# Layer 2 of a two-layer relational graph network on one core: several bunches in one PSUM bank, two banks for the projected sums, and finished blocks in steps

## The chip, the cores and the metric

The kernel runs on one core of one Trainium2 chip. The metric is the device time of one execution in microseconds. The engines are TensorE (PE, with PEld for its weight loads), VectorE (DVE), ScalarE (ACT), GpSimd (POOL, which here only issues gathers) and SyncE (SP, which issues most other transfers). Each engine works through its own instructions in order and waits on semaphores for the others.

## What is computed

12,500 nodes with 128 features, 200,000 edges sorted by destination, ten relations. The relation of an edge is the argmax of ten of its attributes.

```python
def _rgcn_layer(x, src, dst, edge_type, w_rel, root, bias):
    seg = dst * NUM_REL + edge_type
    sums = jax.ops.segment_sum(x[src], seg, num_segments=N * NUM_REL)
    cnt = jax.ops.segment_sum(jnp.ones(seg.shape, x.dtype), seg, num_segments=N * NUM_REL)
    mean = (sums / jnp.maximum(cnt, 1.0)[:, None]).reshape(N, NUM_REL, -1)
    return jnp.einsum('nrd,rdo->no', mean, w_rel) + x @ root + bias
h = jax.nn.relu(_rgcn_layer(x, src, dst, edge_type, w_rel1, root1, b1))
y = _rgcn_layer(h, src, dst, edge_type, w_rel2, root2, b2)
out = _layernorm(x + y, axis=-1)
```

## The kernel before

Layer 1 walks the edges in tiles of 128 and leaves three things in DRAM: `hT` (the hidden features, transposed), `YD` (each node's hidden features already multiplied by the ten relation matrices of layer 2, one row per node and relation), and `SD` (sums of hidden rows by relation and node, for edges that layer 1 itself could serve; they still have to be multiplied by layer 2's matrices). Layer 1 takes about two thirds of the time and isn't touched.

`layer_2` handles the edges that are left: 177 tiles in 45 bunches of up to 4 straight from the edge list ("plain" bunches), then 678 tiles of edges that were compacted meanwhile ("second" bunches of 1, 2 or 4 tiles that share one window of nodes), 261 bunches and 855 tiles in all. The accumulator `acc2` holds 128 features by 12,500 nodes in SBUF. The main loop runs over bunches p, with i counting tiles. In each turn the following is emitted, in this order:

1. DVE makes the weighted one-hot tiles of bunch p + 3 (`hots`, line 840); there are seven one-hot buffers. ACT starts blocks of the accumulator with `h @ root + bias` (`begun`, lines 1499 and 1500), with a PSUM tile `pf` from the pool `ps_f`, which has two buffers.
2. POOL gathers the bunch's rows of `YD`, one indirect transfer of 128 rows per tile (line 833), into six buffers of eight tiles. A buffer can be filled again when PE has read its eight tiles.
3. PE multiplies each gathered tile by its one-hot (line 1607) into the PSUM bank of this bunch: a plain bunch puts its tiles side by side, a second bunch accumulates its tiles on the same columns. Between the matmuls `between` runs what has fallen due at that tile.
4. While the compaction (`brought_together`) is under way, one of its steps.
5. DVE adds bunch p − 2 from its bank into `acc2` at an offset read from a register (line 1637; in the last four turns bunch p − 1).
6. Blocks of 128 or 256 nodes (51 of them, in the order `finals`) to which no later bunch adds are finished: PE transposes them (line 1540), DVE adds x and takes the row statistics (lines 773 to 777), ACT takes the root (line 779), DVE scales (lines 780 and 783), SP stores the rows and loads the x rows of the block three places on, into one of three buffers (line 698).

The banks: three `zy` while the compaction's masks hold three others; once they are closed, two `zq` more, so that bunches take five banks in turn, and one bank `alone`. From then on, every 12 tiles, one of 46 "heavy" blocks gets its part of `SD`: SP loads it (line 1513, 1280 KB, two buffers, the load for block j + 2 issued after the last matmul of block j), PE makes ten matmuls with the relation matrices into `alone` (line 1521, spread over 7 tiles), and DVE adds the result into `acc2` 9 tiles after the first of them (line 1528). A heavy block can be finished only after that.

Of the kernel before, what the change touches and what calls it, by code (L numbers as in the profile page):

```python
# [49 lines left out]
HB = 4  # L50
SPLIT = 64
LEAD = 40
LAST = 40
READY = 5
NEAR = 4
# [13 lines left out]
def rgcn_resnorm_kernel(ctx: ExitStack, tc: tile.TileContext, x, src, dst, attr, w_rel1, root1, b1,  # L69
# [1349 lines left out]
    def layer_2():  # L1419
# [95 lines left out]
        def seen(j, i):  # L1515
            k = heavy[j]
            n0, n, _ = block(k)
            po = alone[0]

            def one(r):  # L1520
                nc.tensor.matmul(po[:, :n], wsb[1][:, r, :], sds[k][:, r, :n], start=(r == 0), stop=(r == NREL - 1))  # L1521
                if r == NREL - 1:
                    sds.pop(k)
                    seen_in(j + 2)

            def added(_):
                assert k in begin[:begins]
                nc.vector.tensor_tensor(acc2[:, n0:n0 + n], acc2[:, n0:n0 + n], po[:, :n], op=ALU.add)  # L1528
# [37 lines left out]
        for p in range(-AH, NB + BE):  # L1566
            if p == plain - AH:
                assert wanted[0] in ready
                masking.close()
                ps_n = fast.enter_context(tc.tile_pool(name="ps_n", bufs=1, space=PSUM))  # L1570
                banks[:] = [next_of("zp", banks) for _ in banks] + [ps_n.tile([P, YB], F32, name=f"zq{j}") for j in range(2)]
                turn_of_["zp"] = 0
                alone.append(ps_n.tile([P, YB], F32, name="alone"))
                for j in range(len(heavy)):
                    seen(j, i + 6 + 12 * j)
            if p + AH < NB:
# [11 lines left out]
            if p < NB:  # L1588
                second, t0, n, w = bunches[p]
                oh = ohs.pop(p)  # L1590
                zps[p] = zp = next_of("zp", banks)
                for j in range(n):
                    if made % GQ == 0:
                        g = next_of("g", gathers)
                        turn = used_[id(g)] = 1 - used_.get(id(g), 1)
                    at = GQ - 1 - made % GQ if turn else made % GQ
                    made += 1
                    t = t0 + j
                    if second:
                        gathered(g, at, YD[:, :], idxB[:, t:t + 1], 1)  # L1600
                    else:
                        gathered(g, at, YD[:NREL * (limit_of(t) + 1), :] if t >= T0 else YD[:, :], idxE[:, t:t + 1], 1)
                    gs[j] = g, at
                for j in range(n):
                    g, at = gs.pop(j)
                    o = 0 if second else j * w
                    nc.tensor.matmul(zp[:, o:o + w], g[:, at * C:(at + 1) * C], oh[:, j * w:(j + 1) * w],  # L1607
                                     start=not second or j == 0, stop=not second or j == n - 1)
                    between.run(issued[p] + j + 1)
                i = issued[p + 1]  # L1610
# [7 lines left out]
            if opened is None and wanted[0] in ready:  # L1618
                opened = i
                for j in range(2):  # L1620
                    seen_in(j)
            for q in [q for q in sorted(zps) if q <= p - (1 if p >= NB - 4 else BE)]:
                second, t0, n, w = bunches[q]
                for j in range(1 if second else n):
                    t = t0 + j
                    if (second, t) not in offs:
# [10 lines left out]
                    nc.vector.tensor_tensor(s, s, zps[q][:, j * w:(j + 1) * w], op=ALU.add)  # L1637
                del zps[q]
            todo.run(i)
            summed_to = min(zps, default=min(p + 1, NB))  # L1640
            while ended < NB2 and done_at[finals[ended]] <= summed_to and (finals[ended] in whole or finals[ended] not in heavy):
                finish(ended)
# [172 lines left out]
```

## Time and profile before

| | us |
|---|---|
| median of three runs | 3691.99 |
| lowest and highest | 3690.94, 3702.55 |
| the profiled execution | 3655.59 |
| its span, first to last instruction | 3653.8 |

The profile is of one execution. It lists for every instruction when it started, how long it took and, where the engine had been idle before, what ended the wait. "Idle before ... <-DVE cc L1528" is a wait that DVE's instruction of line 1528 ended; "issue" is a wait that the profile can't name or the time between instructions; "remote" is a wait that ended with a semaphore whose sender the profile didn't find. A matmul of float32 operands appears as two rows, with a weight load for each. Layer 2's gathers begin at about 2361 us and the last starts at 3618.6 us. In slices of a fortieth of the span (91 us) the page gives PE three to seven tenths after the first slice, DVE mostly three tenths in the last ten slices, and POOL six tenths almost throughout.

### The profile page before, as it was taken

What the parts mean: (1) busy time and instruction counts of PE and PEld (TensorE: products, weight loads), DVE (VectorE), ACT (ScalarE), POOL (GpSimd) and SP (SyncE); (2) the same over time, 40 slices, a digit from 0 to 9 for tenths busy, and PEclk for the clock granted to TensorE, in tenths of its full rate; (3) what the DMA queues carried; (4) which work ended last, traced back from release to release, by engine and by line L of the source; (5) the groups of instructions that cost most, each with busy time, mean ns of one, the idle gap of its engine ahead of it and who ended that gap; (6) DMA issues with size and microseconds to landing.
All of it is one profiled execution on the core that took longest, in us unless ns stands there. A gap on an engine that the chain in (4) does not pass through costs nothing. (4 is left out here: it accounts for less than half of the span.)

```text
span 3653.8 us, 38569 instructions
## 1 busy us (share of the span) xinstructions
PE 2254.1 (62%) x11125; PEld 1859.4 (51%) x11125; DVE 1994.0 (55%) x6434; ACT 514.6 (14%) x799; POOL 2294.6 (63%) x2430
## 2 busy tenths in 40 slices
PE   1556677677676767676667667733556566566534
PEld 0445565565555555555555555623445555555433
DVE  4646576867565757565656565428654333233333
ACT  1111121212121212122212121100000000000000
POOL 5663666666666666666666666566566666666664
PEclk7677877878888888887888877855667777677655
DMA  4553656555555555555656555531144444444322
GB/s 122 154 170 96 189 155 192 153 186 165 172 172 169 172 177 176 171 182 158 191 159 194 158 161 157 146 98 51 46 117 135 143 137 140 136 151 135 97 61 51
DMA packets 376423, 529.31 MB, mean 145 GB/s; under 512 B 55904, under 2 KB 283707, under 8 KB 376204
## 3 DMA queue, kind: packets, MB, share of 16 engines
q0 software_dynamic: 99552, 249.45, 23.9%
q1 hardware_dynamic: 249209, 264.48, 22.4%
q10 hardware_dynamic: 27443, 12.82, 1.2%
q8 instruction: 93, 1.52, 0.2%
q14 instruction: 126, 1.03, 0.1%
HBM read 372.75 MB, written 160.19 MB: 146 GB/s over the span
## 5 line engine op out<-in xcount | busy, mean ns | idle before, releaser
L833 POOL DMA_INDIRECT g<-XH,idxE x1386 | 1314.1, 948 | 737.7 <-issue 364.8
L1077 PEld LDWEIGHTS zp<-oh,g 128*128 128x128 f32 x5898 | 901.7, 229 | 407.3 <-DVE cc L866 201.5
L1077 PE MATMUL zp<-oh,g 128*128 128x120 f32 x5898 | 943.1, 317 | 247.3 <-DVE cc L866 159.0
L866 DVE TENSOR_TENSOR cc<-cc,zp 128x240 f32 (+1 forms) x1563 | 607.1, 388 | 787.1 <-remote 353.0
L833 POOL DMA_INDIRECT g<-YD,idxB x678 | 642.6, 948 | 339.8 <-issue 185.9
L934 PE MATMUL yb<-w,a 128*128 128x512 f32 (+1 forms) x576 | 345.2, 689 | 346.0 <-ACT ys L940 183.1
L840 DVE TENSOR_SCALAR oh<-bank,keyE,wE 128x120 f32<-128x120 f32 x1563 | 517.7, 394 | 0.0
L1521 PE MATMUL alone<-cc,w 128*128 128x256 f32 (+2 forms) x920 | 339.4, 485 | 136.4 <-DVE cc L1528 72.8
L1607 PEld LDWEIGHTS zy<-oh,g 128*128 128x128 f32 x1168 | 245.9, 273 | 222.5 <-DVE cc L1637 155.1
L1607 PE MATMUL zy<-oh,g 128*128 128x12 f32 (+30 forms) x1168 | 237.2, 330 | 197.3 <-DVE cc L1637 148.2
L940 ACT ACTIVATE ys<-yb 128x512 f32<-128x512 f32 (+2 forms) x291 | 153.0, 526 | 1334.4 <-remote 553.7
L934 PEld LDWEIGHTS yb<-w,a 128*128 128x128 f32 x576 | 110.8, 240 | 379.1 <-ACT ys L940 203.6
L1521 PEld LDWEIGHTS alone<-cc,w 128*128 128x128 f32 x920 | 195.3, 247 | 158.3 <-DVE cc L1528 76.5
L826 PE MATMUL pf<-cc,w 128*128 128x256 f32 (+2 forms) x1040 | 248.4, 396 | 15.1 <-issue 9.2
L833 POOL DMA_INDIRECT g<-in_x_dram,idxE x177 | 167.8, 948 | 135.7 <-PE zp L1077 59.3
L833 POOL DMA_INDIRECT g<-YD,idxE x177 | 168.6, 953 | 111.1 <-issue 60.6
L826 PEld LDWEIGHTS pf<-cc,w 128*128 128x128 f32 x1040 | 205.7, 212 | 49.3 <-issue 19.8
L795 ACT ACTIVATE cc<-zero 128x1280 f32<-128x1280 f32 x170 | 214.6, 1262 | 0.0
L840 DVE TENSOR_SCALAR oh<-columns,keyB,wB 128x45 f32<-128x45 f32 (+35 forms) x678 | 177.0, 336 | 0.2 <-issue 0.2
L1637 DVE TENSOR_TENSOR cc<-cc,zy 128x12 f32 (+24 forms) x306 | 58.9, 192 | 177.8 <-remote 145.5
L1607 PEld LDWEIGHTS zq<-oh,g 128*128 128x128 f32 x542 | 113.2, 258 | 30.8 <-issue 18.4
L1528 DVE TENSOR_TENSOR cc<-cc,alone 128x256 f32<-128x256 f32 (+2 forms) x46 | 18.6, 405 | 199.3 <-remote 159.0
(265 smaller groups left out, 1563.5 us busy)
## 6 DMA issues: line engine op xcount, KB each, us to landing
SD<-cc SPq DMA_DIRECT2D x41, 1280.0 KB
cc<-SD SPq DMA_DIRECT2D x41, 1280.0 KB
YD<-ys SPq DMA_DIRECT2D x194, 256.0 KB
m<-in_edge_attr_dram SPq DMA_DIRECT2D x48, 672.0 KB
g<-XH,idxE POOLq DMA_INDIRECT x1386
YD<-ys SPq DMA_DIRECT2D x97, 128.0 KB
XH<-hb SPq DMA_DIRECT2D x44, 256.0 KB
g<-YD,idxB POOLq DMA_INDIRECT x678
```

What stands on the lines that cost most here:

```text
L795: nc.scalar.activation(cc[:, l, h * H:(h + 1) * H, o:o + n], zero[:, None, :n].to_broadcast([P, H, n]), AF.Copy)
L826: nc.tensor.matmul(po[:, :n], wsb[l][:, r, :], sums[:, r], start=(r == 0), stop=(w is None and r == NREL - 1))
L833: nc.gpsimd.indirect_dma_start(out=g[:, j * C:(j + n) * C], out_offset=None, in_=table, in_offset=bass.IndirectOffsetOnAxis(ap=idx, axis=0))
L840: nc.vector.tensor_scalar(oh[:, j * m:(j + 1) * m], cols[:, :m], keys[:, j:j + 1], weights[:, j:j + 1], op0=ALU.is_equal, op1=ALU.mult)
L866: nc.vector.tensor_tensor(s, s, z, op=ALU.add)
L934: nc.tensor.matmul(yb[:h, :m], fin_a[k][:, b * P:b * P + h], wsb[1][:, r:r + m // C, :], start=True, stop=True)
L940: nc.scalar.activation(ys[:h, :m], yb[:h, :m], AF.Copy)
L1077: nc.tensor.matmul(zp[:, o + l * KW:o + (l + 1) * KW], g[:, (slot[j] + l) * C:(slot[j] + l + 1) * C], oh[:, j * KW:(j + 1) * KW], start=Tr ...
L1521: nc.tensor.matmul(po[:, :n], wsb[1][:, r, :], sds[k][:, r, :n], start=(r == 0), stop=(r == NREL - 1))
L1528: nc.vector.tensor_tensor(acc2[:, n0:n0 + n], acc2[:, n0:n0 + n], po[:, :n], op=ALU.add)
L1607: nc.tensor.matmul(zp[:, o:o + w], g[:, at * C:(at + 1) * C], oh[:, j * w:(j + 1) * w], start=not second or j == 0, stop=not second or j = ...
L1637: nc.vector.tensor_tensor(s, s, zps[q][:, j * w:(j + 1) * w], op=ALU.add)
```

## The change

Bunches share a bank. Ahead of the loop a list `bank_of` gives each bunch a bank and its first column there: a bunch goes behind the one before it as long as the bank's 512 columns hold it and it has no more than 8 tiles in all; a new bank is begun at two fixed places and for each of the last four bunches. After the compaction there is one `zq` instead of two, so four banks in turn. Sums of a bunch are now emitted when the bank in use is two further on, among the second bunches two bunches a turn unless the bank is three or more further on, and in the last four turns all at once.

Projected sums use two banks `alone` in turn, and the addition comes 20 tiles after the first matmul instead of 9.

Finishing a block is cut in three steps by tile count: the transposes 8 tiles after the block is complete (and not within 11 tiles of the last block's), the addition of x, the statistics, the root and the x load 9 tiles later, the scaling and the store 4 tiles after that. While the compaction runs, the middle step follows the transposes at once. In the last 32 tiles (`RUSH`) all follow each other at once.

```diff
+        TOGETHER = 8
+        bank_of, cols, tiles = [], YB, 0
+        for p, (second, _, n, w) in enumerate(bunches):
+            m = w if second else n * w
+            if cols + m > YB or tiles + n > TOGETHER or p in (plain - 3, plain) or p >= NB - 4:
+                bank_of.append((bank_of[-1][0] + 1 if bank_of else 0, 0))
+                cols, tiles = m, n
+            else:
+                bank_of.append((bank_of[-1][0], cols))
+                cols, tiles = cols + m, tiles + n
...
-                xbs[finals[j]] = next_of("x", xs)
+                xbs[finals[j]] = xs[j % len(xs)]
...
-            po = alone[0]
+            po = alone[j % 2]
...
-            between.at(i + 9, added)
-
-        def finish(j):
+            between.at(i + 20, added)
+
+        free_from, unscaled = [0], []
+
+        def finish(j, i):
...
-            pr = ps_f.tile([P, 4, C], F32, name="pf")
-            for b, h in subs:
-                nc.tensor.transpose(pr[:h, b, :], acc2[:, n0 + b * P:n0 + b * P + h], ident)
-            normed(k, xbs.pop(k), pr, (next_of("v", vs), next_of("o", os_)))
-            rows_in_turn(j + 3)
+            held = {}
+
+            def turned_rows(i):
+                held["pr"] = pr = ps_f.tile([P, 4, C], F32, name="pf")
+                for b, h in subs:
+                    nc.tensor.transpose(pr[:h, b, :], acc2[:, n0 + b * P:n0 + b * P + h], ident)
+                del pr
+                if jobs.due or i >= NG - RUSH:
+                    measured(i)
+                else:
+                    todo.at(i + 9, measured)
+
+            def measured(i):
+                while unscaled:
+                    unscaled[0](i)
+                pr, xb = held.pop("pr"), xbs.pop(k)
+                held["v"] = v = next_of("v", vs)
...
+                for p, s in spans(k):
+                    nc.vector.tensor_tensor(v[:p, s], pr[:p, s], xb[:p, s], op=ALU.add)
...
+                for p, s in spans(k):
+                    nc.scalar.activation(rstd[:p, s], mv[:p, s, 1], AF.Sqrt, bias=eps[:p])
+                rows_in_turn(j + 3)
+                unscaled.append(scaled)
+                if i < NG - RUSH:
+                    todo.at(i + 4, scaled)
+                else:
+                    scaled(i)
+
+            def scaled(_):
...
+                for p, s in spans(k):
+                    nc.vector.reciprocal(rstd[:p, s], rstd[:p, s])
...
+                rows_dma(o, out, k, True)
+
+            if i >= NG - RUSH:
+                todo.run(END)
+                turned_rows(i)
+            else:
+                at = max(i + 8, free_from[0])
+                free_from[0] = at + 11
+                todo.at(at, turned_rows)
...
-                banks[:] = [next_of("zp", banks) for _ in banks] + [ps_n.tile([P, YB], F32, name=f"zq{j}") for j in range(2)]
+                banks[:] = [next_of("zp", banks) for _ in banks] + [ps_n.tile([P, YB], F32, name="zq")]
...
-                alone.append(ps_n.tile([P, YB], F32, name="alone"))
+                alone += [ps_n.tile([P, YB], F32, name=f"alone{j}") for j in range(2)]
...
-                zps[p] = zp = next_of("zp", banks)
+                zp, col = zps[p] = (next_of("zp", banks) if not bank_of[p][1] else zps[p - 1][0]), bank_of[p][1]
...
-            for q in [q for q in sorted(zps) if q <= p - (1 if p >= NB - 4 else BE)]:
+            if p >= NB - 4:
+                due = [q for q in sorted(zps) if q < p]
+            else:
+                due = [q for q in sorted(zps) if bank_of[q][0] <= bank_of[p][0] - 2]
+                if p >= plain:
+                    due = due[:max(2, sum(bank_of[q][0] <= bank_of[p][0] - 3 for q in due))]
+            for q in due:
...
-                    nc.vector.tensor_tensor(s, s, zps[q][:, j * w:(j + 1) * w], op=ALU.add)
-                del zps[q]
+                    nc.vector.tensor_tensor(s, s, zp[:, col + j * w:col + (j + 1) * w], op=ALU.add)
```

More of the change, by code (lines that the diff above doesn't have):

```diff
@@ L52 @@
 LEAD = 40
+RUSH = 32
 LAST = 40
@@ new lines, in measured @@
+            def measured(i):
[3 more added lines that the diff above has]
+                held["v"] = v = next_of("v", vs)
+                held["mv"] = mv = small.tile([P, 4, 2], F32, name="mv")
+                held["rstd"] = rstd = small.tile([P, 4], F32, name="rstd")
+                for p, s in spans(k):
+                    nc.vector.tensor_tensor(v[:p, s], pr[:p, s], xb[:p, s], op=ALU.add)
+                for b, h in subs:
+                    st = small.tile([P, nc.vector.BN_STATS_DIM], F32, name="st")
+                    nc.vector.bn_stats(st[:h], v[:h, b, :])
+                    nc.vector.bn_aggr(mv[:h, b, :], st[:h])
+                for p, s in spans(k):
[6 more added lines that the diff above has]
+                    scaled(i)
@@ new lines, in scaled @@
+            def scaled(_):
+                if scaled not in unscaled:
+                    return
+                unscaled.remove(scaled)
+                v, mv, rstd = (held.pop(a) for a in ("v", "mv", "rstd"))
+                o = next_of("o", os_)
+                for p, s in spans(k):
+                    nc.vector.reciprocal(rstd[:p, s], rstd[:p, s])
+                for b, h in subs:
+                    nc.vector.tensor_scalar(o[:h, b, :], v[:h, b, :], mv[:h, b, 0:1], rstd[:h, b:b + 1],
+                                            op0=ALU.subtract, op1=ALU.mult)
+                rows_dma(o, out, k, True)
@@ L1605, in layer_2 @@
                     g, at = gs.pop(j)
-                    o = 0 if second else j * w
+                    o = col if second else col + j * w
                     nc.tensor.matmul(zp[:, o:o + w], g[:, at * C:(at + 1) * C], oh[:, j * w:(j + 1) * w],
@@ L1621, in layer_2 @@
                     seen_in(j)
-            for q in [q for q in sorted(zps) if q <= p - (1 if p >= NB - 4 else BE)]:
+            if p >= NB - 4:
[5 more added lines that the diff above has]
+            for q in due:
                 second, t0, n, w = bunches[q]
+                zp, col = zps.pop(q)
                 for j in range(1 if second else n):
@@ L1641, in layer_2 @@
             while ended < NB2 and done_at[finals[ended]] <= summed_to and (finals[ended] in whole or finals[ended] not in heavy):
-                finish(ended)
+                finish(ended, i)
                 ended += 1
```

## The prediction

> **What bounds the kernel now.** I read the page first, then the busy time of all engines in stretches of layer 2 (only its code changes), then the waits of each engine there, then the timeline around one stop.
>
> ```profile
> span 3653.8 us, 38569 instructions
> ## 1 busy us (share of the span) xinstructions
> PE 2254.1 (62%) x11125; PEld 1859.4 (51%) x11125; DVE 1994.0 (55%) x6434; ACT 514.6 (14%) x799; POOL 2294.6 (63%) x2430
> ```
>
> No engine is full. The stretches of layer 2 tell more (busy us and instructions of PE, PEld, DVE, ACT, POOL; all of POOL's are gathers):
>
> ```profile
> core 0: us, PE busy (x) PEld busy (x) DVE busy (x) ACT busy (x) POOL busy (x), PEclk, DMA share, GB/s
> 2388.00:2602.00 214.00, 72.39 (x290) 62.61 (x290) 133.32 (x341) 8.85 (x24) 141.18 (x148) 0.50 0.26 66
> 2602.00:2746.00 144.00, 87.92 (x393) 74.25 (x393) 79.89 (x369) 7.05 (x18) 83.23 (x88) 0.71 0.31 89
> 2746.00:3488.70 742.70, 446.89 (x2043) 386.97 (x2043) 249.51 (x1089) 25.59 (x69) 485.36 (x512) 0.72 0.45 133
> 3488.70:3619.60 130.90, 52.43 (x228) 48.33 (x227) 41.25 (x183) 2.36 (x8) 90.08 (x95) 0.50 0.24 61
> 3619.60:3653.80 34.20, 13.64 (x58) 11.98 (x58) 19.11 (x81) 2.07 (x7) 0.00 (x0) 0.50 0.16 33
> ```
>
> Time per gather: 214.0/148 = 1.446 us, 144.0/88 = 1.636, and in the long third stretch 742.7/512 = 1.451. There DVE is busy a third of the time and PE 60%. What POOL does between its gathers stands in its group for that stretch, and the stops themselves in its timeline:
>
> ```profile
> L833 POOL DMA_INDIRECT g<-YD,idxB x513 | 486.3, 948 | 260.9 <-issue 140.1 <-remote 84.9 <-PE zy L1607 18.1
> ```
> ```profile
> 2386.81 0.95 POOL L833 DMA_INDIRECT g<-YD,idxE  x1 [11.16 <-issue]
> ...
> 2450.39 0.94 POOL L833 DMA_INDIRECT g<-YD,idxE  x1 [7.46 <-remote]
> ...
> 3304.62 0.95 POOL L833 DMA_INDIRECT g<-YD,idxB  x1 [3.30 <-remote]
> ...
> 3488.83 0.95 POOL L833 DMA_INDIRECT g<-YD,idxB  x1 [3.18 <-PE zy L1607]
> ...
> 3522.89 0.95 POOL L833 DMA_INDIRECT g<-YD,idxB  x1 [4.27 <-remote]
> ```
>
> A gather takes 0.95 us and 0.30 of issue, so 1.25 in a row; the rest of the idle time, 260.9 − 140.1 = 120.8 us, is stops. From 3488.83 to 3522.89 are 34.06 us: 24 gathers (30.0) and a stop that costs 4.27 − 0.30 = 3.97 more. From 2386.81 to 2450.39 are 45 gathers and a stop of 7.46. The commonest run is 16 gathers: 20.0 + 3.0 = 23.0. So a stop grows with the run before it: 16 gathers cost 1.4375 us each, 24 cost 1.4154, 45 cost 1.25 + 7.16/45 = 1.409. What a stop is, one of them shows, with all engines:
>
> ```profile
> 3267.35 0.66 PE L1521 MATMUL alone<-cc,w 128*128 128x256 f32 x2
> ...
> 3268.00 0.66 PE L1499 MATMUL pf<-cc,root 128*128 128x256 f32 x2
> ...
> 3277.26 0.95 POOL L833 DMA_INDIRECT g<-YD,idxB  x1 [0.31 <-issue]
> 3281.33 0.52 SPq L1513 DMA_DIRECT2D cc<-SD  x1
> 3281.34 0.42 DVE L1528 TENSOR_TENSOR cc<-cc,alone 128x256 f32<-128x256 f32 x1 [13.80 <-remote]
> 3281.42 0.47 ACT L1500 ACTIVATE cc<-pf,b 128x256 f32<-128x256 f32 x1 [19.01 <-remote]
> 3281.61 0.95 POOL L833 DMA_INDIRECT g<-YD,idxB  x1 [3.40 <-remote]
> ```
>
> PE has finished line 1521's last matmul by 3268.0 and line 1499's by 3268.7. ACT, SP, DVE and POOL, which wait for these or for later ones, all go on at 3281.3 to 3281.6, about 13 us after the matmuls and 3 us after POOL's last gather. **PE's word that a matmul is done reaches the others late while POOL gathers back to back, and at once when POOL has stopped.** "Remote" is how the profile names it. Who loses by it, in the long stretch:
>
> ```profile
> DVE cc L1528 <- remote: 135.4, 13, 14.5
> DVE cc L1637 <- remote: 106.1, 15, 12.5
> DVE cc L773 <- remote: 72.2, 9, 15.2
> ```
> ```profile
> PE alone L1521 <- DVE cc L1528: 72.8, 11, 12.6
> ```
>
> DVE stands 313.7 us in front of the three operations that the change postpones; PE, out of one-hot tiles or of the bank `alone`, stands behind DVE. PE therefore advances only some 16 tiles per stop, and POOL, whose six gather buffers of 8 tiles PE must free, gets 16 gathers.
>
> **The change, part by part.** No part adds or drops an arithmetic instruction, a transfer or a byte; all move waits. Sums per tile are as before (171 in the long stretch, below).
>
> *Shared banks.* Before, bunch q is added up two bunches later, which by the loop is 6 tiles after its matmuls, and five banks of one bunch hold about 5 × 3.0 = 15 tiles. After, four banks of up to 8 tiles hold up to 32, and a sum comes, by the same loop, 9 to 18 tiles later, 12 in the mean.
>
> ```profile
> 2746.00:3488.70 742.70, 39.34 (x171) 0.72 0.45 133
> ```
>
> 512 gathers over these 171 additions of line 1637 is 3.0 tiles a bunch. At 1.45 us a tile the slack goes from 9 to 17 us, against waits of at most 12.5. In the first two stretches (three banks) the same holds, 8 tiles instead of 4 a bank.
>
> *Two `alone` banks, addition at 20 instead of 9.* Ten matmuls lie within 7 tiles, so DVE's slack goes from 3 tiles (4 us) to 14 (20 us), and PE still has 4 tiles before the bank comes round at 24. Waits were up to 14.5 us: they mostly go.
>
> *Finished blocks in steps.* Before, DVE waits for transposes issued just before: no slack. After, 9 tiles (13 us), and 4 more behind ACT's root. Behind the waiting DVE instruction stand the next one-hot tiles, then PE. On SP the x load now comes 9 tiles later and the store 13, in its one queue with the SD loads.
>
> ```profile
> SPq L698 <- DVE o L783: 60.5, 14, 18.3
> ```
>
> SP stands 60.5 us of the long stretch before such a store; standing further back, the stores hold it less. The x load has two blocks' time (51 blocks to 855 tiles, so 2 × 17 × 1.45 = 49 us); without that cover its 128 KB would cost DVE under 1 us at the rate shown under (b). I take 0 for both. `pf`, with two buffers, is held for 9 tiles; the other one serves line 1499, once in about 16 tiles.
>
> **What is late next.** With the last word from PE at tile S, DVE now gets to S + 9 or more, where it got to S + 0 (a block), + 3 or + 6; three bunches of one-hots carry PE 9 further. So PE gains some 8 tiles a stop, one gather buffer: **runs of 24 instead of 16**, 1.4154 us a gather. Longer runs hardly add: the 45 gathers bound it at 1.409. Stops don't vanish, because POOL needs PE's word too.
>
> The sum, against the profiled execution's 3655.59 us (1.8 outside its span):
> - long stretch: 512 × 1.4154 = 724.7, **−18.0**. Bounds: −6.7 (512 × 1.4375, only stops above 3.3 us go) and −21.3 (1.409).
> - 2388 to 2602: at 1.4154, 209.5, so −4.5 at most; DVE is busy 133 of 214 us with the list of the second half, which isn't touched. I take **−2**.
> - 2602 to 2746: at 1.4154, 124.6, so −19.4 at most, 0 at least; PE and DVE work there on that same list one after the other. Nearest to the stretch before: **−3**.
> - 3488.7 to 3619.6: runs are 24 already, **0**.
> - the end:
>
> ```profile
> 3622.04 0.42 DVE L773 TENSOR_TENSOR cc<-pf,x 128x256 f32<-128x256 f32 x1 [22.52 <-remote]
> ...
> 3625.70 2.00 PE L1607 MATMUL zy<-oh,g 128*128 128x82 f32 x8 [15.98 <-DVE cc L1637]
> ```
>
> DVE waits through the whole last run, and when it ends PE has 25 of the 855 tiles left (its 58 rows in the last stretch above, less 8 of transposes, two rows a tile). After, the last 32 tiles finish at once, as now, but by the loop the block in question comes 12 tiles later, and the one-hots with it. PE took some 14 us for the 25, from 3625.7 to 3639.9: 12 tiles less are −7 at most; I take **−3**, as the sums and blocks behind them stay.
>
> Sum −26: 3629.6 for an execution like the profiled one. The median of the runs shown is 3691.99, 36.4 above it; I take the same 26 off: **3666**.
>
> **Rivals.**
> (a) *Runs stay at 16*, because another chain of PE's word has less slack than I think (ACT's line 1499/1500, the 9 tiles of a block). Then −6.7, and 1 at the most elsewhere: **3684**. For it: ACT waited 19.01 us above.
> (b) *Slower: the SD loads come late.* SP issues the load for block j + 2 only on PE's word that block j is done, and PE needs it 17 tiles (24 us) later.
>
> ```profile
> DMA packets 928, 0.98 MB, mean 328 GB/s; under 512 B 16, under 2 KB 912, under 8 KB 928
> ```
> ```profile
> SPq L1513 <- remote: 253.6, 18, 19.0
> ```
>
> Between 3260 and 3263 one load flows at 328 GB/s: 1280 KB take 4 us, say 6 with its start, which leaves 18. The run quoted began 23 us before 3281.6, and the first late matmul ended at 3268.0, 9 us on; in a run and stop of 34 us the word can be late by 25. So a block that ends in the first 7 us of that time, 7/34 of 43, hence 8 or 9 loads, has its load up to 7 us late, and PE starts again only after it. From 3.1 us each it eats the 26; at 5 us each (+42) it gives **3708**.
> (c) *Stops vanish*: PE keeps close to the gathers, and its word, even late, comes before POOL needs it, six buffers on. Then 1.25 a gather: 120.8 of the long stretch, **3571**. Against it: the run of 45 ended in the longest stop of all.
> (d) *Banks count, not tiles.* The Trainium skill, Perfetto Trace Analysis, "Matmuls" under "Optimizing Tensor Performance", says that independent matmul groups should rotate through different PSUM banks so that emptying one overlaps the next; here a bunch no longer gets its own. As a mechanism of this kernel: four banks for bunches instead of five put PE behind DVE's sums, as three banks did before 2746. Half-way from 1.451 to the 1.517 of the first two stretches together (358.0/236) is +0.033 a gather, +17: **3709**. Against it: the sums of a bank are 12 tiles old when they are read, and PE's wait is for the one-hots and `alone`.
>
> **How the numbers follow.** Forecast 0.56, (a) 0.21, (b) 0.12, (c) 0.06, (d) 0.05. All bounds of the sum together are −52, 3640. The range goes from 3636 to 3706, leaving out (c), (d) and the worse half of (b). 0.3%, about what a measurement of this kernel can tell from no change, is 11 us: faster 0.62 (forecast, (c)), same 0.21, slower 0.17.
>
> **What would show it.** After: POOL's stops some 34 us apart and near 4.3 us; the DVE rows "L1528, L1637, L773 <- remote" well under the 313.7 us; 512 gathers of the long stretch in about 725 us. Stops still 23 us apart make (a) right; PE standing before line 1521 with SP's SD load just landed, (b); runs of 40 and more without a stop of 6 us, (c). The forecast is wrong at its root if PE's word is no longer late, or is late without regard to POOL's runs.

## The result, and the profile after

Before 3691.25 us, after 3701.57 us (medians of 12 runs each); the ratio is 1.0022, with a 95% interval of 1.0012 to 1.0032. The change makes no gain; it costs some 8 us. Forecast were 26 us less.

The profiled execution of the kernel after took 3693.38 us. Its page, and the stretches of layer 2 between the same gathers as in the prediction (columns as there):

```profile
span 3691.6 us, 38716 instructions
PE 2319.4 (63%) x11125; PEld 1901.6 (52%) x11125; DVE 1995.1 (54%) x6434; ACT 513.8 (14%) x799; POOL 2287.9 (62%) x2430
```
```profile
2409.00:2623.40 214.40, 69.56 (x294) 63.40 (x295) 125.81 (x329) 7.49 (x23) 140.32 (x148) 0.50 0.26 66
2623.40:2774.30 150.90, 94.00 (x390) 78.56 (x390) 87.06 (x383) 8.48 (x19) 83.19 (x89) 0.68 0.30 88
2774.30:3522.40 748.10, 480.96 (x2063) 405.16 (x2062) 248.78 (x1083) 24.99 (x67) 483.88 (x512) 0.70 0.44 131
3522.40:3656.10 133.70, 49.96 (x207) 47.19 (x208) 44.10 (x192) 2.36 (x8) 88.97 (x95) 0.50 0.23 60
3656.10:3691.60 35.50, 14.00 (x58) 12.04 (x57) 18.60 (x77) 2.36 (x8) 0.94 (x1) 0.50 0.18 40
```

The 512 gathers of the long stretch take 748.1 us, where 724.7 were forecast. (Executions differ by several us a stretch; a pair taken together is below.) Its waits in that stretch (us in total, times, longest), and POOL's group of gathers:

```profile
DVE cc L1707 <- remote: 103.7, 12, 13.6
PE alone L1533 <- issue: 102.1, 104, 2.6
DVE oh L841 <- remote: 91.7, 22, 11.6
PE zy L1670 <- issue: 82.5, 88, 2.5
DVE cc L1572 <- remote: 36.0, 6, 13.4
PE zq L1670 <- issue: 27.5, 23, 2.6
DVE cc L1540 <- remote: 14.4, 1, 14.4
```
```profile
L834 POOL DMA_INDIRECT g<-YD,idxB x512 | 483.9, 945 | 271.0 <-issue 143.8 <-remote 52.2 <-PE zy L1670 27.4
```

Lines 1707, 1540 and 1572 are the sums, the addition of `alone` and the first step of a block, which were 1637, 1528 and 773: their 313.7 us have become 154.1. PE's 72.8 us in front of the addition are 1.2. So the waits that the change was aimed at are half gone. (These rows are the waits called remote. With those that the profile puts down to some PE row, DVE's idle time before the three operations went from 462.9 us to 274.3, and before the one-hot tiles from 0.2 to 167.5; all its idle time in the stretch is 493 us in both.) In their place stand DVE in front of the one-hot tiles (line 841, 91.7 us) and PE with 212.1 us of "issue": time in which it waited for nothing that the profile shows. POOL's idle time is no shorter. Its stops, from its timeline:

```profile
3103.01 0.94 POOL L834 DMA_INDIRECT g<-YD,idxB  x1 [3.61 <-remote]
...
3126.38 0.94 POOL L834 DMA_INDIRECT g<-YD,idxB  x1 [3.71 <-PE alone L1533]
```

They lie 23.4 us apart, 16 gathers, as before: 29 of the 34 runs between stops in the long stretch have 16. What PE's issue time looks like, its timeline shows. POOL took up gathering at 3149.95 us:

```profile
3159.35 0.66 PE L1533 MATMUL alone<-cc,w 128*128 128x256 f32 x2
3159.85 0.32 PE L1670 MATMUL zy<-oh,g 128*128 128x50 f32 x2
3160.01 0.40 PE L1557 MATMUL pf<-ident,cc 128*128 128x128 f32 x2
3160.24 0.60 PE L1511 MATMUL pf<-cc,root 128*128 128x256 f32 x2
3160.68 0.41 PE L1670 MATMUL zy<-oh,g 128*128 128x51 f32 x2
3161.60 0.30 PE L1670 MATMUL zy<-oh,g 128*128 128x51 f32 x1 [0.51 <-issue]
3163.01 0.24 PE L1670 MATMUL zy<-oh,g 128*128 128x51 f32 x1 [1.12 <-issue]
3164.41 0.45 PE L1670 MATMUL zy<-oh,g 128*128 128x51 f32 x1 [1.16 <-issue]
3165.81 0.24 PE L1670 MATMUL zy<-oh,g 128*128 128x51 f32 x1 [0.95 <-issue]
3167.24 0.24 PE L1670 MATMUL zy<-oh,g 128*128 128x51 f32 x1 [1.19 <-issue]
3168.67 0.43 PE L1670 MATMUL zy<-oh,g 128*128 128x51 f32 x1 [1.18 <-issue]
```

From 3156 to 3161 us PE begins five or six rows in each us. Then it begins one row every 1.4 us, though DVE had made the four one-hot tiles of these rows by 3157.9 us and their gathers had been issued some 50 us earlier. Two rows belong to a tile, and the second, which needs nothing that the first didn't, comes 1.4 us behind it too, which a late word can't explain. **PE crawls.** The experiments ask what makes it crawl and what that is worth.

### The profile page after: what moved, and what is told of

Same layout as the page of the kernel before. It is cut to its first block, busy times and chain, and to the rows that moved or that the text cites. A ratio compares the mean times of both kernels' runs of the same rounds, so it can differ in the third digit from the quotient of the medians.

```text
span 3691.6 us, 38716 instructions
## 1 busy us (share of the span) xinstructions
PE 2319.4 (63%) x11125; PEld 1901.6 (52%) x11125; DVE 1995.1 (54%) x6434; ACT 513.8 (14%) x799; POOL 2287.9 (62%) x2430
## 5 line engine op out<-in xcount | busy, mean ns | idle before, releaser
L1078 PEld LDWEIGHTS zp<-oh,g 128*128 128x128 f32 x5898 | 914.2, 232 | 398.8 <-issue 177.4
L1078 PE MATMUL zp<-oh,g 128*128 128x120 f32 x5898 | 953.1, 319 | 230.4 <-DVE cc L867 135.8
L935 PE MATMUL yb<-w,a 128*128 128x512 f32 (+1 forms) x576 | 359.9, 716 | 380.5 <-ACT ys L941 206.5
L1670 PEld LDWEIGHTS zy<-oh,g 128*128 128x128 f32 x1366 | 296.3, 275 | 280.0 <-issue 149.6
L1670 PE MATMUL zy<-oh,g 128*128 128x12 f32 (+33 forms) x1366 | 285.6, 330 | 240.1 <-issue 130.4
L1533 PE MATMUL alone<-cc,w 128*128 128x256 f32 (+2 forms) x920 | 357.2, 493 | 104.5 <-issue 102.1
L827 PEld LDWEIGHTS pf<-cc,w 128*128 128x128 f32 x1040 | 209.4, 215 | 57.7 <-issue 23.3
L1707 DVE TENSOR_TENSOR cc<-cc,zy 128x12 f32 (+21 forms) x339 | 64.7, 196 | 253.2 <-remote 94.3
L1512 ACT ACTIVATE cc<-pf,b 128x256 f32<-128x256 f32 (+2 forms) x51 | 23.7, 465 | 700.1 <-remote 313.1
L1670 PEld LDWEIGHTS zq<-oh,g 128*128 128x128 f32 x344 | 75.1, 264 | 57.6 <-issue 47.9
```

What stands on the lines that cost most here:

```text
L827: nc.tensor.matmul(po[:, :n], wsb[l][:, r, :], sums[:, r], start=(r == 0), stop=(w is None and r == NREL - 1))
L935: nc.tensor.matmul(yb[:h, :m], fin_a[k][:, b * P:b * P + h], wsb[1][:, r:r + m // C, :], start=True, stop=True)
L1078: nc.tensor.matmul(zp[:, o + l * KW:o + (l + 1) * KW], g[:, (slot[j] + l) * C:(slot[j] + l + 1) * C], oh[:, j * KW:(j + 1) * KW], start=Tr ...
L1512: nc.scalar.activation(acc2[:, n0:n0 + n], po[:, :n], AF.Identity, bias=bsb[1])
L1707: nc.vector.tensor_tensor(s, s, zp[:, col + j * w:col + (j + 1) * w], op=ALU.add)
```

## The experiments

Five theories stood against each other. *Q*: slack counts, but whole buffers of 8 tiles round it down. *O*, and more widely *W*: another wait for PE's word, the one-hot tiles first, binds at 16. *F*: runs of any length cost the same. *C*: PE's crawl binds. *E*: each PE instruction puts a fixed time into POOL's stops. Further on: *R*, any short rest of POOL cures it, and *P*, what PE gets is in proportion to the rest. The table is all runs that follow. The long stretch is from the 249th gather of layer 2 to the 761st, from the trace; the runs are those in it between stops of over 0.5 us; "over 1.25" is (stretch − 512 × 1.25) / 512, the time in which POOL doesn't gather, for each gather; the end is from the last gather's start to the span's end.

| kernel | commonest runs | long stretch us | over 1.25 | end us | ratio to before [95%] |
|---|---|---|---|---|---|
| e1_before | 28 of 16 | 740.2 | 0.196 | 36.7 | one run |
| e1_after | 29 of 16 | 742.1 | 0.199 | 34.9 | one run |
| e1_release4 | 31 of 12 | 741.9 | 0.199 | 34.2 | 1.0012 [1.0000, 1.0025] |
| e1_hots13 | 29 of 16 | 738.8 | 0.193 | 30.4 | 1.0003 [0.9992, 1.0014] |
| e2_after_one | 15 of 16, 9 of 24 | 738.7 | 0.193 | 34.1 | 0.9994 [0.9983, 1.0006] |
| e2_before_one | 14 of 24, 9 of 16 | 730.1 | 0.176 | 26.7 | 0.9980 [0.9965, 0.9995] |
| e2_after_narrow | 29 of 16 | 742.3 | 0.200 | 34.9 | 1.0017 [1.0006, 1.0028] |
| e2_after_unread | see below | 706.8 | 0.130 | 58.5 | 1.0768 [1.0746, 1.0790] |
| e3_banks | 26 of 16, 12 of 8 | 748.1 | 0.211 | 36.3 | 1.0018 [1.0008, 1.0029] |
| e3_steps | 30 of 16 | 744.2 | 0.204 | 37.9 | 1.0008 [0.9999, 1.0017] |
| e3_alone | 30 of 16 | 744.3 | 0.204 | 38.2 | 1.0003 [0.9993, 1.0012] |
| e3_pause | rests of 1.82 us | 749.7 | 0.214 | 17.7 | 0.9975 [0.9965, 0.9986] |
| e4_pause_before | rests of 1.82 us | 748.8 | 0.213 | 18.5 | 0.9995 [0.9981, 1.0009] |
| e4_pause1k_after | rests of 0.97 us | 739.9 | 0.195 | 35.3 | 1.0010 [0.9994, 1.0026] |
| e4_pause1k_before | rests of 0.97 us | 741.0 | 0.197 | 35.6 | 1.0009 [0.9998, 1.0020] |
| e4_pause512_after | rests of 0.54 us | 741.3 | 0.198 | 31.2 | 0.9998 [0.9984, 1.0012] |
| e5_pause1664 | rests of 1.50 us | 741.1 | 0.197 | 24.4 | 0.9990 [0.9979, 1.0002] |
| e5_pause1792 | rests of 1.61 us | 741.7 | 0.199 | 18.2 | 0.9966 [0.9952, 0.9980] |

Each group (e1 to e5) ran on one chip, with the kernel before beside it.

**Both kernels as they are, on one chip.**

> The kernel before, unchanged, on the same chip as the three that follow, to have its trace beside theirs. If the longer stops seen after the change (3.65 us behind 16 gathers instead of 3.30) belong to the chip or the execution, this trace has stops near 3.65 us too where the next one has; if they belong to the change, it has 3.30 while the kernel after has 3.65.

> The kernel after, unchanged, on the same chip. Both theories: within 0.3% of the kernel before. Its stops behind 16 gathers are as long as those of the kernel before (theory: the chip sets them) or 0.3 us longer (theory: the change does).

3660.43 and 3658.31 us. The median of the stops behind 16 gathers is 3.41 us before and 3.47 after, so the 3.69 us in the first trace of after belong to the chip or the execution, not to the change. The stretches before and after: 217.0 and 210.5; 144.2 and 148.7; 740.2 and 742.1; 129.8 and 131.3; 36.7 and 34.9. Two small gains and three small losses, −0.4 in sum. The long stretch of the kernel before:

```profile
2751.90:3492.10 740.20, 433.32 (x2040) 375.14 (x2041) 249.07 (x1088) 25.50 (x69) 483.67 (x513) 0.73 0.43 134
```
```profile
PE alone L1521 <- DVE cc L1528: 83.0, 12, 15.0
PE alone L1521 <- issue: 51.8, 31, 9.0
PE pf L1540 <- DVE cc L1637: 47.7, 6, 15.0
PE zy L1607 <- issue: 41.7, 35, 2.2
PE pf L1540 <- issue: 34.1, 11, 10.7
```

And of the kernel after:

```profile
2748.10:3490.20 742.10, 476.90 (x2053) 396.68 (x2053) 251.14 (x1084) 25.07 (x67) 483.53 (x512) 0.70 0.43 131
```
```profile
PE alone L1533 <- issue: 98.1, 94, 2.6
PE zy L1670 <- issue: 67.9, 75, 2.9
PE zq L1670 <- issue: 45.6, 46, 2.5
```

PE lost 130.7 us of waiting for DVE, and its issue time went from 127.6 to 211.6 in these rows. Most of what the change gave PE, the crawl took; PE's busy time rose too, from 433.3 to 476.9 us for as many rows, at a granted clock of 0.70 instead of 0.73. Counted from the start of each run of 16 gathers in the kernel after, PE begins 7.4, 6.6, 9.6, 10.8, 11.0, 6.4, 3.1, 2.1, 1.3, 1.6 and 1.5 rows in each 2 us that follow (means of 29 runs): brisk for some 11 us, then a crawl until POOL stops. In the kernel before they are 7.9, 7.3, 8.2, 9.8, 9.6, 5.7, 3.2, 2.0, 1.7, 2.0 and 2.1 (28 runs). In these 22 us PE begins 61.5 rows after the change and 59.6 before it: the slack brought it hardly any.

**Smaller releases, more one-hot tiles.** e1_release4 lets the gather buffers go by 4 tiles; e1_hots13 has 13 one-hot tiles, made 5 bunches ahead.

```diff
+        GQ = 4
+        gathers[:] = [g[:, j * GQ * C:(j + 1) * GQ * C] for g in gathers for j in range(2)]
+        turn_of_["g"] = 0
```
```diff
+                at0 = 2 * NREL * BN
+                hots_[:] = [next_of("oh", hots_) for _ in hots_] + [every[:, at0 + j * YB:at0 + (j + 1) * YB] for j in range(6)]
+                turn_of_["oh"] = OB
+                ahead = 5
...
-            if p + AH < NB:
+            while hotted <= min(p + ahead, NB - 1):
```

> The kernel after with layer 2's gather buffers let go by 4 tiles instead of 8 (twelve half buffers, the same memory). Theory Q: PE now gets some 17 to 21 tiles on per stop, and the whole buffers of 8 round this down to 16. Then runs of 20 gathers appear, stops are some 28.5 us apart in the long stretch, and the time falls by some 0.1 to 0.3% against the kernel after (20 gathers with a stop by the line through 3.30 and 4.27 us: 1.425 us a gather instead of 1.4375, some 6 us). Theory O (the one-hot tiles alone hold PE at 16): runs of 16 stay. Theory F (runs of any length cost the same): runs of 20, and no gain.

> The kernel after with 13 one-hot tiles instead of 7 from the opening of the second half on, made 5 bunches ahead instead of 3. Theory O (the one-hot tiles are the next chain that waits for PE's word): DVE's waits for line 841, 91.7 us in the long stretch, go to below 20, runs of 24 gathers become the commonest, and the time falls by 0.3 to 0.5% against the kernel after. Theory Q (several chains have a slack of 17 to 21 tiles, and buffers of 8 round it down): the waits for line 841 go, other waits for PE's word take their place (line 1572, SP's line 1525), runs of 16 stay the commonest, time within 0.2%.

Runs of 12, not 20: Q falls. With 13 one-hot tiles DVE's waits at line 841 have no row left in that stretch; the sums (line 1713 there) wait instead, and the runs and the stretch stay:

```profile
2751.50:3490.30 738.80, 470.14 (x2066) 395.58 (x2066) 246.88 (x1091) 24.83 (x67) 483.87 (x512) 0.71 0.43 132
```
```profile
DVE cc L1713 <- remote: 190.5, 22, 16.9
PE alone L1533 <- issue: 90.1, 85, 2.6
```

O falls too. And with stops of 2.69 us behind 12 gathers or 3.47 behind 16, the stretch is the same.

**Less work for PE.** One of the ten matmuls of a heavy block, in both kernels; or ten of 64 columns.

```diff
-                nc.tensor.matmul(po[:, :n], wsb[1][:, r, :], sds[k][:, r, :n], start=(r == 0), stop=(r == NREL - 1))
+                nc.tensor.matmul(po[:, :n], wsb[1][:, r, :], sds[k][:, r, :n], start=True, stop=True)
...
-            for r in range(NREL):
-                between.at(i + 2 * r // 3, lambda _, r=r: one(r))
+            between.at(i + 2 * (NREL - 1) // 3, lambda _: one(NREL - 1))
```
```diff
-                nc.tensor.matmul(po[:, :n], wsb[1][:, r, :], sds[k][:, r, :n], start=(r == 0), stop=(r == NREL - 1))
+                nc.tensor.matmul(po[:, :min(n, 64)], wsb[1][:, r, :], sds[k][:, r, :min(n, 64)], start=(r == 0), stop=(r == NREL - 1))
...
-                nc.vector.tensor_tensor(acc2[:, n0:n0 + n], acc2[:, n0:n0 + n], po[:, :n], op=ALU.add)
+                m = min(n, 64)
+                nc.vector.tensor_tensor(acc2[:, n0:n0 + m], acc2[:, n0:n0 + m], po[:, :m], op=ALU.add)
```

> The kernel after with one of the ten matmuls of line 1533 for each of the 43 or so heavy blocks; the other nine relations of those blocks are left out of the result. Theory C (TensorE itself crawls: once POOL has gathered for some 11 us without a stop, PE lets about one row go per us whatever it waits for, so the 63 rows that 16 tiles need fill the time of 16 gathers): with 39 rows per 16 tiles PE gets further per stop, runs of 24 and more become the commonest and the long stretch falls from 742 to about 725 us. Theory W (what binds is how much slack the waits for PE's word have, and PE is fast enough): the waits are the same, runs of 16 stay, the stretch stays within 6 us of 742. Theory E (each PE instruction puts a fixed 0.04 us into POOL's stops): 774 matmul rows fewer take some 31 us off, 711 us, stops after 16 gathers below 2.5 us.

> The kernel before with the same nine of ten matmuls left out (the bank alone is still one, with its addition 9 tiles on). It tells what the change is worth where PE has room. Theory C: some waits for PE's word come back as the bound, runs of 16 and 24 mixed, the stretch between 728 and 740 us, and slower than the kernel after with the same matmuls left out. Theory W: as slow as the kernel before whole, 740 us. Theory E: as fast as the kernel after with the same matmuls left out.

> The kernel after with all ten matmuls of line 1533, each over 64 of its 256 columns; the other columns of those blocks are left out of the result. The number of PE's instructions is that of the kernel after, its busy time is less by some 0.16 us for each of the 860 rows. Theory C, if the crawl starts after a number of instructions: runs stay at 16 and the stretch near 742 us. Theory C, if it starts after a time: PE does more rows in the fast 11 us, runs of 24, about 725 us. Theory W: 742 us.

The long stretches of these three, in that order:

```profile
2745.00:3483.70 738.70, 325.60 (x1267) 290.87 (x1267) 248.60 (x1072) 25.07 (x67) 484.25 (x513) 0.51 0.43 132
```
```profile
2753.10:3483.20 730.10, 309.09 (x1275) 275.86 (x1275) 248.15 (x1082) 25.51 (x69) 483.78 (x513) 0.53 0.43 134
```
```profile
2751.10:3493.40 742.30, 472.80 (x2054) 451.00 (x2054) 244.69 (x1083) 24.95 (x67) 484.25 (x513) 0.51 0.42 131
```

With 1270 rows instead of 2050 the runs of 24 come, 9 and 14 of them, in the kernel before too, which has none of the change's slack. So how many gathers PE keeps up with per stop hangs on how much PE must put through for them, and not on slack: W falls in both kernels, and C holds for the runs. Whether it is the number of rows or their time, the third kernel doesn't tell. Its rows of line 1533 took 400 ns instead of 482 in the mean, but the granted clock was 0.51 instead of 0.70, the rows into `zy` took 402 ns instead of 304, and PE was busy for 472.8 us, as with the whole matmuls (476.9). For the time C doesn't hold: for the kernel after 725 us were expected and 738.7 came; for the one before 728 to 740, and more than for the kernel after, and 730.1 came, which is less. E falls by more (711 expected): some 775 rows fewer took 3.4 us off the kernel after and 10.1 off the one before (by the traces of the first group), not 31. Longer runs bring little, and the lightened kernel after is slower than the lightened one before.

**POOL that never waits for PE.**

```diff
-                    nc.tensor.matmul(zp[:, o:o + w], g[:, at * C:(at + 1) * C], oh[:, j * w:(j + 1) * w],
+                    nc.tensor.matmul(zp[:, o:o + w], ident if p >= plain else g[:, at * C:(at + 1) * C], oh[:, j * w:(j + 1) * w],
```

> The kernel after whose second-half matmuls of line 1670 read a constant tile and not the gathered one; all gathers are still issued, the sums are those of the constant. POOL then waits for nothing of PE in the second half. If the 0.17 us that each gather adds to the next stop is work of POOL's own path that must be done some time, gathers come no faster than 1.41 us each, 512 in about 722 us. If it is only the time by which PE's word is late, POOL never stops: 1.25 us each, 640 us, and PE crawls through the whole of it, its matmuls ending long after the last gather.

POOL gathers at 1.25 us each for 175 on end, then, behind a stop of 37.83 us for the list that DVE makes, for 178: for that long nothing in its own path makes it stop, and 16 are far fewer. After each of these it gets slower by itself, with rows of 1.09 us and a gather every 1.40:

```profile
3441.49 1.09 POOL L834 DMA_INDIRECT g<-YD,idxB  x1 [0.30 <-issue]
3442.89 1.09 POOL L834 DMA_INDIRECT g<-YD,idxB  x1 [0.31 <-issue]
```

So the 512 gathers take 706.8 us, neither the 640 nor the 722 of the expectation; what slows POOL isn't known. The rest of the core comes to a halt meanwhile, and at the end POOL stands 296.25 us behind DVE. Three windows of 100 us, of gathering at 1.25, at 1.40, and of that last stop:

```profile
3200.00:3300.00 100.00, 9.30 (x22) 5.83 (x21) 7.91 (x37) 0.47 (x1) 75.62 (x81) 0.50 0.19 53
3440.00:3540.00 100.00, 15.32 (x35) 10.36 (x36) 3.94 (x14) 0.77 (x2) 75.88 (x71) 0.50 0.21 61
3600.00:3700.00 100.00, 99.86 (x626) 92.00 (x625) 71.02 (x316) 8.73 (x24) 0.00 (x0) 1.00 0.68 216
```

22 rows of PE beside 81 gathers, 35 beside 71, 626 beside none; of DVE 37, 14 and 316. What the two engines wait for while POOL gathers, the longest row of each from 2745 to 3460 us tells:

```profile
PE pf L1511 <- issue: 221.6, 7, 82.8
DVE dn L1381 <- remote: 150.7, 2, 77.3
```

PE is held without a wait that the profile shows. DVE waits for words; that its own instructions are held isn't shown. The stops that POOL makes for PE's word are when the others do most of their work; without them the kernel takes 7.7% longer.

**The parts of the change alone**, each put into the kernel before (the diff's own lines; with two `alone` banks the bunches have four banks, not five).

> The kernel before with the shared banks alone: four banks of up to 8 tiles, sums two banks later; one bank alone with its addition 9 tiles on; blocks finished at once. Theory C (PE gets a set number of rows per stop; moved waits gain nothing): the long stretch within 4 us of the kernel before's 740; if the shared banks bring what was seen elsewhere after the change, the stretch from the 13th to the 161st gather is 4 to 6 us shorter and the one from there to the 249th 4 to 6 us longer, and the whole within 0.2% of the kernel before. Theory W (slack counts, and the weakest of the three waits decides): same, as lines 1528 and 773 still wait.

> The kernel before with the finished blocks in steps alone (9 and 4 tiles between). Theory C: long stretch within 4 us of 740, whole within 0.2%. If the steps are what lengthens the stretch of the list's making after the change (the two pf banks are held 9 tiles while that list takes them too), that stretch is 4 to 8 us longer here and not with the shared banks alone.

> The kernel before with two banks alone in turn and the addition 20 tiles on; the bunches have four banks of their own instead of five, as PSUM has no ninth. Theory C: PE's 72.8 us in front of line 1521 go, and as much comes back as issue time of PE and as waits for the fourth bank; the long stretch is within 4 us of 740, whole within 0.2%. Theory W: a few us shorter.

The stretches from the 13th gather on are 213.5, 149.3, 748.1 and 132.5 us with the banks, 218.0, 141.7, 744.2 and 130.2 with the steps, 216.9, 143.0, 744.3 and 130.4 with `alone`. Each part takes its own waits away and they come back at the other two: the three lines of before have together 317.9 us of "remote" in e1_before, 328.9 with the banks, 334.5 with the steps, 292.0 with `alone`. The shared banks seem to carry what the change costs: 1.0018, where the intervals of the other two parts hold 1, and by stretch the change's own shape: beside the other two parts some 4 us less in the first and 6 to 8, 4 and 2 more in the next three. Why they cost it isn't settled; the waits name no bank that PE stood for.

**POOL made to rest.** A clearing of a buffer that nothing reads, behind every eighth gather of the second half. First in the kernel after, then in both, then shorter.

```diff
+        idle = every[:, 2 * NREL * BN:2 * NREL * BN + 2048]
...
                     gs[j] = g, at
+                    if p >= plain and made % 8 == 0:
+                        nc.gpsimd.memset(idle, 0.0)
```

> The kernel after in which POOL clears 2048 columns of a buffer that nothing reads behind every eighth gather of the second half (some 2 us in which it gathers nothing). If it is gathering without a stop that makes PE crawl, PE's issue waits in the long stretch, 225 us, fall below 80 us, POOL's stops for PE's word go (all below 1 us beside the clearing), and the stretch is some 64 times the clearing longer than 640 us, so 770 to 800 us. If PE crawls for a reason of its own, its issue waits stay above 180 us and POOL's stops stay beside the clearing.

```profile
PE zy L1673 <- DMA g<-YD,idxB: 84.0, 65, 4.8
PE alone L1534 <- issue: 23.3, 36, 1.8
```

PE's issue time in front of `alone` is 23.3 us instead of 98.1, POOL has no other stop, and PE now waits for gathers to land: at a gather of the long stretch it is 8.7 tiles behind in the mean, against 33.8 in e1_after. That is gathering making PE crawl, not PE. The stretch is 749.7 us all the same, less than the 770 to 800 expected, as a clearing adds only 1.69 us to the usual 0.30 between gathers (in this group, where the stops behind 16 gathers are longer, 3.50 us in e3_alone and 3.56 in e3_steps, it was 744 without the rest), but the end is 17.7 us instead of 35, as PE has 3 tiles left at the start of the last gather and not 24 or 25.

> The kernel before with POOL clearing 2048 columns (1.82 us) behind every eighth gather of the second half, as was done to the kernel after. It tells what the change is worth where POOL's gathers no longer hold PE and its word back. If slack for PE's word then counts, PE's waits for line 1528 remain here (over 40 us), POOL has stops beside the clearing, and the long stretch is 5 to 20 us longer than with the change (749.7). If the clearing alone cures it, the stretch is within 3 us of that and the change is worth nothing there either.

> The kernel after with 1024 columns (about 0.95 us) behind every eighth gather. Theory R (any rest of about 1 us in 10 is enough to let PE's word and PE's instructions through): no other stops, 8 gathers in 11.0 us, the long stretch 700 to 712 us, the whole some 50 us faster than the kernel after. Theory P (what PE gets is in proportion to the rest): PE falls behind again, stops for PE's word of over 1 us come back beside the clearing, the stretch is between 730 and 760 us.

> The kernel before with 1024 columns behind every eighth gather. Theory R: as the kernel after with it, if the change is worth nothing; 5 to 25 us longer in the long stretch if, with PE let through, the slack of the change counts. Theory P: 730 to 760 us.

> The kernel after with 512 columns (about 0.5 us) behind every eighth gather. Theory R, if half a microsecond is enough: 8 gathers in 10.5 us, 672 to 685 us. Theory P: the runs of 8 join again to 16 and 24 with stops of 3 us, the stretch near 742 us.

With the rest, the kernel before has the same stretch as the kernel after, 748.8 and 749.7, close to what POOL's gathers and clearings make by themselves (640 + 64 × 1.69 = 748): PE keeps up in both, and the slack is worth nothing there either. (The ratios, 0.9995 and 0.9975, are of two groups. From the 13th gather on the two traces take 1263 and 1265 us, so layer 2 gives no reason for that difference.) R falls: with rests of 0.97 and 0.54 us the stops for PE's word come back beside the clearing, and the stretch stays at 740 to 741 us, as P says.

> The kernel after with 1664 columns behind every eighth gather, by 0.97 us for 1024 and 1.82 us for 2048 some 1.50 us, so 1.36 us of rest more than the 0.30 of issue. The stops of before grow by 0.17 us for each gather, 1.32 us for eight. If that is a debt to be paid whatever the order, this rest just pays it: no other stops, 8 gathers in 11.4 us, the long stretch 725 to 732 us, PE close behind the gathers at the end (the time behind the last gather 18 us instead of 35), and the whole 0.5 to 0.9% below the kernel before. If more rest is needed, stops for PE's word return, the stretch stays at 738 to 745 us and the end at 30 us or more.

> The kernel after with 1792 columns behind every eighth gather, some 1.61 us, so 1.47 us of rest more than the issue. By the same debt of 1.32 us: no other stops, the long stretch 732 to 740 us, the end 18 us, the whole 0.4 to 0.7% below the kernel before. If stops for PE's word return here too, the debt is above 1.47 us for eight gathers.

The two rows of the last kernel, long stretch and end:

```profile
2744.20:3485.90 741.70, 526.39 (x2056) 425.93 (x2054) 290.12 (x1096) 24.92 (x67) 587.27 (x577) 0.69 0.43 131
3619.50:3637.70 18.20, 3.45 (x10) 2.09 (x10) 5.84 (x24) 1.18 (x4) 0.94 (x1) 0.50 0.24 38
```

The expected debt of 0.165 us a gather was too small. With rests of 1.50 us 18 of the 75 in and after the long stretch are lengthened by over 0.1 us, with 1.61 us 11, and both stretches come out at 741 us again. Whatever share of it the rest doesn't pay, a stop pays: some 0.198 us for each gather, worked out as (741.4 − 640) / 512. Eleven kernels of the table, with runs of 8, 12, 16 and 24 and waits in quite different places, have the stretch between 738.7 and 742.3 us. F, put this way, fits best, with exceptions: e2_before_one paid 0.176, and the kernels of the third group, without rests, 0.204 to 0.211. What sets the figure is open. It isn't POOL's own debt, as e2_after_unread gathers 175 times without paying, and it isn't PE's rows alone, as e2_after_one has some 790 fewer and pays 0.193. DVE begins between 1044 and 1096 instructions in the long stretch of each of the eleven; whether their number sets it wasn't tried. With 1.61 us the debt is just paid by the end, PE is caught up (3 tiles left), and the kernel is 0.34% faster than before (0.20 to 0.48%); a gain of the size of the end's 17 us.

## Why the prediction was wrong, point by point

*PE's word is late while POOL gathers.* Right, and not enough: PE's own instructions are held as well (22 rows in 100 us beside gathers, 626 beside none).

*The waits for lines 1528, 1637 and 773 go.* Partly right: 135.4 to 14.4 us and 72.2 to 36.0, but the sums' 106.1 are 103.7, and 91.7 us appeared at the one-hot tiles.

*"So PE gains some 8 tiles a stop, one gather buffer: runs of 24 instead of 16."* This is the step that failed. It took what PE gets done per stop for a matter of whom it waits for. The runs showed that it is a matter of how much PE gets through before the crawl: some 60 rows per run of 16, before the change (59.6) and after it (61.5); 13 one-hot tiles left 29 runs of 16; 775 rows fewer brought runs of 24, without the change as well; and where the rests lift the crawl, the stretches before and after are equal.

*"1.4154 us a gather."* Also wrong, by itself. The stop behind a run was read as 0.17 us a gather and a fixed part that longer runs spread. With 14 runs of 24 the stretch came to 730.1 us, 1.426 a gather, and in most kernels to some 1.445 to 1.450, whether POOL stopped after 8, 12 or 16.

*The terms.* On one chip: −18.0 us forecast for the long stretch, +1.9 measured; −2 and −6.5 for the first; −3 and +4.5 for the second; 0 and +1.5; −3 and −1.8 at the end. The first stretch fell by more than said and the end by less; they don't make up for the rest.

*The rivals.* (a) had the sign: stops still 23 us apart. Its price, −6.7, didn't come, since shorter stops are no gain while the debt stays. (b) is not seen: no row of PE's waits in the long stretch of the kernel after names an SD load. (c) is not seen in any kernel that waits for PE. (d) is left with a grain: the shared banks alone are slower, by 0.0018 × 3682.58 = 6.6 us against the 17 of the rival, but with them, and in the kernel after, no row shows PE behind DVE's sums for want of a bank. It does stand so in e3_alone, where four banks hold one bunch each: 34.7 us before `zq` (line 1607) behind line 1637.

## What to carry to other kernels

Before giving an engine more slack, look whether it uses the time it has: rows of an engine that begin at an even, slow beat with "issue" ahead of them may be held by something that no slack cures, here the gathers. Where an engine's idle time stays the same in total while its waits change places, suspect a cost of the work itself, and ask what else it delays; here it was the backlog behind the last gather, and taking the same idle time in small rests took some 17 us off the end. A stop that grows with the run before it isn't by itself a saving to be had from longer runs: work out the mean over the stretch first.

## What the runs showed of the hardware

While POOL issues indirect gathers without a break (0.95 us and 0.30 of issue each), the other engines almost stand still: 22 rows of PE and 37 instructions of DVE in 100 us, against 626 and 316 beside no gathers. Behind a stop of 3.4 us PE runs freely for some 11 us; then, beside rows that follow at once, the gaps from row to row are 0.7, 1.4, 2.1 and 2.8 us, most often 1.4, with no wait that the profile shows. A clearing of 1.82 us on POOL behind every eighth gather lifts it, so it is the gathers and not POOL's being busy. After some 175 gathers without a stop, in e2_after_unread alone, POOL's own rows lengthen from 0.95 to 1.09 us.

For each gather of layer 2 the trace has 16 packets of 4096 bytes and 16 of 4 bytes, and the last ends some 2.1 us after the gather's start where nothing else is moved. The Trainium skill, Perfetto Trace Analysis, "DMA Instruction — SWDGE (GPSIMD)", says that the row of such an instruction ends when its descriptors are written, and that each DMA engine's last descriptor writes the semaphore; the trace agrees, with rows of 0.95 us and the first packet some 1.65 us after the row's start. Whether the words and instructions of the others queue behind these 16 writes wasn't tried, and no run here shows it.

The stops behind 16 gathers differ between groups of runs: their median is 3.41 us and 3.47 in the kernels before and after taken together, 3.50 and 3.56 in e3_alone and e3_steps, 3.69 in the first trace of the kernel after. A term of 0.1 us a stop, some 3 us a stretch, is no more than that.
